# An audio tower on one core: feature-major tensors by batch, folds in place, residual from ScalarE, other buffers at the end

## Chip, cores and metric

The kernel runs on one core of one Trainium2 chip. The metric is device time in microseconds, from the runs of the whole kernel; the profile is that of one further execution. Engines are named as in the profile: PE (TensorE, matmuls), DVE (VectorE), ACT (ScalarE), POOL (GpSimd), SP (SyncE, which here issues DMAs).

## What is computed

64 recordings of 80,000 samples are cut into 157 frames of 512 samples. Each frame is turned by an orthonormal cosine transform (DCT); then come one attention-like layer and one layer of experts, each with a layernorm before it and a residual around it. Cut to what matters:

```python
h = einsum('bfh,kh->bfk', frames, DCT)                   # 64 x 157 x 512
x = layernorm(h)
key, qry = exp(1j*pi*tanh(x @ Wk)), exp(1j*pi*tanh(x @ Wq))   # 4 sets x 8 planes
V = x @ Wv + bv
total = sum over sets: softmax(set_weights)[s] * Re(conj(qry_s) . cumsum_t(key_s * V))
pos   = the same with fixed phases pos * pos_freqs
gate  = sigmoid(x @ Wg + bg)
total = gate * total + (1 - gate) * sigmoid(pos_weight) * pos
h = h + x + (total / norm(t)) @ Wo + bo
y = layernorm(h)
e = argmax_e softmax(mean_t(y) @ rWg + rbg)              # one expert of 16 for a recording
h = h + gate_e * (y @ We[e] + be[e])
```

The cumulative sums are computed as masked products of phases: with 157 positions, scores of 157 x 157 for each recording.

## The kernel before

**Tiles.** The 64 recordings go in 16 groups of 4. A group's 4 x 157 tokens (padded to 160) make five tiles of 128 partitions (NM = 5): four head tiles with the first 128 tokens of one recording each, and one tail tile with the last 32 of all four, of which 29 count (LT). Token-major tiles are 128 x 512; feature-major tensors, which matmuls need as moving or stationary operand, are turned by PE transposes: `transpose_tile` (lines 106 to 111) makes four of them into one PSUM bank and ACT copies the bank into columns of `xT` (L111). Before the change `xT` has 640 columns for each of four feature chunks: 512 of the heads (HEADS) and then 128 of the tails (TAILS).

**Stages of a group g.** `embed` (136 to 165) makes a frame tile into h and x: `fold` (113 to 122) adds and subtracts the mirrored quarters of a frame (`even`, `odd`, then `twice`: L118, L120 and L121 on DVE, L119 on POOL), which halves the DCT's matmuls (L151, L153); `layernorm` (94 to 104) takes the statistics on DVE (L97, L99), the square root on ACT (L101), and then the reciprocal and x on DVE (L103, L104). L157 makes the residual h + x on DVE out of PSUM, and L158 adds the output bias on POOL. `values` (167 to 176) makes V. `phases` (276 to 293) makes keys and queries: 8 matmuls with the weights standing and 512 or 128 columns moving (L284), tanh, sine. `gates` (295 to 312) is the same with 4 x 8 matmuls of 512 or 116 columns (L306) and a sigmoid after each half (L311). `attend` (314 to 369) makes scores (L320, L325), the weighted sums (L345 of 314 columns, L354), the gating (L330, L331), the output product (L131 with `wo`), the residual (L364) and the second layernorm. `turn_x2` (371 to 376) transposes that into `x2T`, of which there is one buffer. `pick` (378 to 445) sums the router's logits over tokens (L388, L396), chooses an expert on DVE, and has POOL gather four weight matrices of 1 MB (L437). `experts` (447 to 484) multiplies (L131, and L465 for the tail tile, four narrow column groups side by side), adds a gathered bias (L453, L473), scales, adds the residual (L476) and writes: L480 for a head tile, 128 rows, and L483 for the tail tile, four DMAs of 29 rows each.

**What sets the order.** Each engine works through its queue in order, and so does SP, which issues all plain DMAs. The engines' order isn't the text's alone: Tile builds it, and moves instructions up where their operands allow it. Buffers come from rings: PSUM has three pairs of banks (`psum`, tag mm) and two single banks (`bank`, tag tr); `frame` has 5 buffers, `even` one, `odd` and `twice` two, `x` three (shared with the outgoing `o`), `we` four, `be` two. A write into a ring's buffer waits for the last reader of what was there. So the frame loads of group g+2 (L81) go out as soon as the folds of group g+1 have read their frames, while PE is in the gates and the attention of group g; `embed(g+1)` is interleaved there with `gates(g)` and `attend(g)`, a tile at a time:

```python
        phases(g)
        next(picks, None)
        if g > 0:
            done(values(g))
        done(picks)
        next(ahead, None)
        for _ in gates(g):
            next(ahead, None)
        attend(g, ahead)
```

The experts of group g-1 follow, then `turn_x2(g)`. At the end (lines 509 to 518) the experts of group 14 begin with the tail tile, then `turn_x2(15)` and `pick(15)` are called between its tiles, and `experts(15)` takes tiles 0 to 3 and then the tail tile.

Of the kernel before, what the change touches and what calls it, by code (L numbers as in the profile page):

```python
# [13 lines left out]
F32 = mybir.dt.float32  # L14
# [7 lines left out]
P = 128  # L22
C = D // P
GB = 4
# [5 lines left out]
HEADS, TAILS = slice(0, GB * P), slice(GB * P, NM * P)  # L30
# [9 lines left out]
def audio_tower(ctx: ExitStack, tc: tile.TileContext, a, out):  # L40
# [16 lines left out]
    small = pool("small", 4)  # L57
# [8 lines left out]
    def psum():  # L66

        return ps_mm.tile([P, 2, 512], F32, tag="mm", name="mm")
# [25 lines left out]
    def layernorm(x, h):  # L94

        st = small.tile([P, 6], F32, tag="st", name="st")
        nc.vector.bn_stats(st, h)  # L97
        mv = small.tile([P, 2], F32, tag="mv", name="mv")
        nc.vector.bn_aggr(mv, st)  # L99
        sd = small.tile([P, 1], F32, tag="sd", name="sd")  # L100
        nc.scalar.activation(sd, mv[:, 1:2], AF.Sqrt, bias=eps)  # L101
        rstd = small.tile([P, 1], F32, tag="rstd", name="rstd")
        nc.vector.reciprocal(rstd, sd)  # L103
        nc.vector.tensor_scalar(x, h, mv[:, 0:1], rstd, ALU.subtract, ALU.mult)  # L104

    def transpose_tile(xT, m, x):

        tr = bank()
        for c in range(C):
            nc.tensor.transpose(tr[:, c * P : (c + 1) * P], x[:, c * P : (c + 1) * P], ident)  # L110
        nc.scalar.copy(xT[:, :, m * P : (m + 1) * P], tr.rearrange("p (c t) -> p c t", c=C))  # L111

    def fold(ft):

        even = p1.tile([P, 2, P], F32, tag="even", name="even")
        odd = p2.tile([P, 2, P], F32, tag="odd", name="odd")
        twice = p2.tile([P, 2, P], F32, tag="twice", name="twice")
        nc.vector.tensor_tensor(even, ft[:, :2, :], ft[:, 2:, :], ALU.add)  # L118
        nc.gpsimd.tensor_tensor(odd, ft[:, :2, :], ft[:, 2:, :], ALU.subtract)  # L119
        nc.vector.tensor_tensor(twice[:, 0, :], even[:, 0, :], even[:, 1, :], ALU.add)  # L120
        nc.vector.tensor_tensor(twice[:, 1, :], even[:, 0, :], even[:, 1, :], ALU.subtract)  # L121
        return twice, odd
# [13 lines left out]
    def embed(g):  # L136


        xT = p1.tile([P, C, NM * P], F32, tag="xT", name="xT", bufs=2)
        res = []  # L140
        pending = None
        S[g] = dict(xT=xT, res=res)
        folded = {0: fold(frames.pop((g, 0)))}
        for m in range(NM):
            h = psum()[:, 0, :]
            twice, odd = folded.pop(m)
            if m + 1 < NM:
                folded[m + 1] = fold(frames.pop((g, m + 1)))
            quarter = h.rearrange("p (r j) -> p r j", r=4)
            for i in range(2):  # L150
                nc.tensor.matmul(quarter[:, 2 * i, :], twice[:, i, :], dct_e[:, i, :], start=True, stop=True)  # L151
            for i in range(2):
                nc.tensor.matmul(quarter[:, 1::2, :], odd[:, i, :], dct_o[:, i, :], start=(i == 0), stop=(i == 1))  # L153
            x = p2.tile([P, D], F32, tag="x", name="x", bufs=3)
            layernorm(x, h)
            r = p1.tile([P, D], F32, tag="res", name="res", bufs=3 * NM)
            nc.vector.tensor_tensor(r, h, x, ALU.add)  # L157
            nc.gpsimd.tensor_tensor(r, r, bo, ALU.add)  # L158
            res.append(r)
            if pending is not None:  # L160
                transpose_tile(xT, *pending)
            pending = (m, x)
            yield
        transpose_tile(xT, *pending)
        yield

    def values(g):

        s = S[g]
        s["v"] = []  # L170
        for m in range(NM):
            ps = by_tokens(psum()[:, 0, :], lambda c: s["xT"][:, c, m * P : (m + 1) * P], wv)
            vt = p1.tile([P, D], F32, tag="v", name="v", bufs=NM)
            nc.vector.tensor_tensor(vt, ps, bv, ALU.add)  # L174
            s["v"].append(vt)
            yield


    first = embed(0)
# [65 lines left out]
    kf = const.tile([P, NM * P], F32, name="kf", tag="kf")  # L245
    qf = const.tile([P, GB, LP], F32, name="qf", tag="qf")
    nc.gpsimd.memset(kf[2 * F :], 0.0)
    nc.gpsimd.memset(qf[2 * F :], 0.0)
    rows = slice(2 * F, 2 * F + 2 * PLANES)
    for i in range(GB):  # L250
        nc.vector.tensor_copy(kf[rows, i * P : (i + 1) * P], pf[:, :P])
        nc.vector.tensor_copy(kf[rows, GB * P + TL * i : GB * P + TL * (i + 1)], pf[:, P:])
        nc.vector.tensor_scalar(qf[rows, i, :], pf, sigp[: 2 * PLANES], -1.0, ALU.mult, ALU.mult)
# [21 lines left out]

    def phases(g):

        xT = S[g]["xT"]
        u = p1.tile([P, NM * P], F32, tag="tT", name="u")
        ps = psum()  # L280
        for k, cols in enumerate((HEADS, TAILS)):
            n = cols.stop - cols.start
            for c in range(C):
                nc.tensor.matmul(ps[:, k, :n], wkq[:, c, :], xT[:, c, cols], start=(c == 0), stop=(c == C - 1))  # L284
            nc.scalar.activation(u[:, cols], ps[:, k, :n], AF.Tanh, bias=bkq)
        nc.vector.scalar_tensor_tensor(u, u, sgn, u, ALU.mult, ALU.max)
        rows = slice(0, 2 * F)
        nc.scalar.activation(kf[rows], u[rows], AF.Sin, bias=off[rows], scale=scl[rows])
        rows = slice(2 * F, P)
        for cols, t, at in ((HEADS, P, slice(0, P)), (TAILS, TL, slice(P, LP))):  # L290
            ub = u[rows, cols].rearrange("p (b t) -> p b t", t=t)
            nc.scalar.activation(qf[: 2 * F, :, at], ub, AF.Sin, bias=off[rows], scale=scl[rows])
        nc.vector.tensor_scalar(qf[: 2 * F], qf[: 2 * F], wvec, None, ALU.mult)

    def gates(g):

        s = S[g]
        xT = s["xT"]
        s["gT"] = gT = p1.tile([P, C, GB, LP], F32, tag="gT", name="gT")
        for o in range(C):  # L300
            ps = psum()
            for k in range(2):
                for c in range(C):
                    moving = xT[:, c, HEADS] if k == 0 else by_tail(xT[:, c, TAILS])
                    n = GB * P if k == 0 else GB * LT
                    nc.tensor.matmul(  # L306
                        ps[:, k, :n], wg[:, c, o * P : (o + 1) * P], moving, start=(c == 0), stop=(c == C - 1)
                    )
                t, at = (P, slice(0, P)) if k == 0 else (LT, slice(P, L))
                pb = ps[:, k, :n].rearrange("p (b t) -> p b t", t=t)  # L310
                nc.scalar.activation(gT[:, o, :, at], pb, AF.Sigmoid, bias=bg[:, o : o + 1])  # L311
            yield

    def attend(g, between):
# [5 lines left out]
        nc.tensor.matmul(ps[:, :P], kf[:, TAILS], qf[:, :, P:], start=True, stop=True)  # L320
        nc.vector.tensor_tensor(tails[:, :, 0, :], by_tail(ps[:, :P]), mask_t, ALU.mult)

        def scores(i):
            ps = bank()
            nc.tensor.matmul(ps[:, :L], kf[:, i * P : (i + 1) * P], qf[:, i, :L], start=True, stop=True)  # L325
            nc.vector.tensor_tensor(att[i % 2][:, 0, :], ps[:, :L], mask, ALU.mult)  # L326
# [41 lines left out]
        for k in ("xT", "v", "gT"):  # L368
            del s[k]

    def turn_x2(g):

        s = S[g]
        s["x2T"] = xT = p1.tile([P, C, NM * P], F32, tag="x2T", name="x2T")
        for m in range(NM):
            transpose_tile(xT, m, s["x2"][m])

    def pick(g):
# [5 lines left out]
        for part, n, first in ((ps[:, :P], P, 0), (ps[:, P:L], LT, GB * P)):  # L384
            for c in range(C):
                for b in range(GB):
                    at = first + b * (P if first == 0 else TL)
                    nc.tensor.matmul(  # L388
                        part[TL * b : TL * (b + 1)],
                        rwg[:, c, :],  # L390
                        xT[:, c, at : at + n],
                        start=(c == 0),
                        stop=(c == C - 1),
                    )
# [52 lines left out]
    def experts(g, order):  # L447
# [3 lines left out]
        for m in order:  # L451
# [8 lines left out]
            if m < GB:  # L460
                by_tokens(ps, lambda c: xT[:, c, m * P : (m + 1) * P], ws[m])
            else:
                for c in range(C):
                    for i in range(GB):
                        nc.tensor.matmul(  # L465
                            ps[TL * i : TL * (i + 1), :],
                            xT[:, c, GB * P + TL * i : GB * P + TL * (i + 1)],
# [11 lines left out]
            if m < GB:  # L479
                nc.sync.dma_start(out=out[GB * g + m, :P, :], in_=o)  # L480
            else:
                for i in range(GB):
                    nc.sync.dma_start(out=out[GB * g + i, P:, :], in_=o[TL * i : TL * i + LT, :])  # L483
# [5 lines left out]
    for g in range(NG):  # L489
# [4 lines left out]
        phases(g)  # L494
        next(picks, None)
# [22 lines left out]
    done(experts(NG - 1, range(NM)))  # L518
# [92 lines left out]
```

## Time and profile before

| | us |
|---|---|
| median of 3 runs | 1660.39 (1660.22 to 1661.74) |
| the profiled execution, device time | 1660.9 |
| its span, first to last instruction | 1659.1 |
| PE busy | 1592.7 |
| DVE busy | 937.4 |
| ACT busy | 545.1, of which table loads at L101 119.3 and at L311 98.8 |
| POOL busy | 326.6 |
| a middle group (638.20 to 738.73) | 100.53 |
| in it, DCT of the next group, gates and attention (738.73 to 779.40) | 40.67, PE busy 38.98 |

The profile gives for each group of instructions the line, the engine, output and inputs by name, the shape, the count, the busy time, the mean of one, and the idle time before it with what ended it. Ends of matmuls are modelled, so the spacing of their starts says more than their busy time. `mm<-wv,xT` reads: tile mm written from wv and xT. A wait is written as who waited, for whom: total us, times, longest. The timeline gives start, length, engine, line, count; SPq and POOLq are the queues that only issue. In the table by windows the columns are the length, then the busy time and the count of PE, weight loads, DVE, ACT and POOL, the granted PE clock, the busy share of the 16 DMA engines, and GB/s.

### The profile page before, as it was taken

To read this page: it belongs to the slowest core of one execution; us is meant where nothing else is said; L and a number is where in the kernel's file an instruction comes from. 1 tells how busy PE (TensorE), PEld (TensorE's weight loads), DVE (VectorE), ACT (ScalarE), POOL (GpSimd) and SP (SyncE) were. 2 spreads that over 40 slices of the span, in tenths; PEclk is the share of its full clock that TensorE was granted. 3 is DMA by queue.
4 is the path that set the end of the run, shared out by engine and by line. 5 is a ranking of instruction groups with operands and counts; after the bars stand their busy time and mean duration, and the time that the engine had idled before them with its cause. 6 is when DMAs were issued, how large, how long until landed. Compare 5 with 4: busy or idle time off the path is not lost. (4 is left out here: it accounts for less than half of the span.)

```text
span 1659.1 us, 18042 instructions
## 1 busy us (share of the span) xinstructions
PE 1592.7 (96%) x6724; PEld 875.5 (53%) x6724; DVE 937.4 (56%) x2162; ACT 545.1 (33%) x769; POOL 326.6 (20%) x377
## 2 busy tenths in 40 slices
PE   7999999999999999999999999999999999999984
PEld 4555556464554645556454554645546455564531
DVE  6556647466463755747466474755637556464452
ACT  3634143251522515134250432515224251342110
POOL 3203112031120403103031120312104031030102
PEclk9999999999999999999999999999999999999997
DMA  5104113141211413013141121413114130121314
GB/s 188 32 1 146 31 56 110 51 146 45 104 48 51 146 48 136 25 45 140 51 146 36 64 97 51 146 45 116 36 51 146 49 136 18 36 112 51 114 50 164
DMA packets 41206, 135.40 MB, mean 82 GB/s; under 512 B 6224, under 2 KB 6624, under 8 KB 32544
## 3 DMA queue, kind: packets, MB, share of 16 engines
q0 software_dynamic: 15616, 88.09, 15.3%
q1 hardware_dynamic: 25504, 46.17, 8.2%
q8 instruction: 53, 0.87, 0.2%
q14 instruction: 33, 0.27, 0.0%
HBM read 113.67 MB, written 20.58 MB: 81 GB/s over the span
## 5 line engine op out<-in xcount | busy, mean ns | idle before, releaser
L306 PE MATMUL mm<-xT,wg 128*128 128x512 f32 (+1 forms) x1024 | 299.9, 438 | 10.0 <-DVE res L157 9.1
L131 PE MATMUL mm<-wv,xT 128*128 128x512 f32 x640 | 283.9, 598 | 3.6 <-ACT xT L111 3.6
L131 PE MATMUL mm<-we,x2T 128*128 128x512 f32 x512 | 225.2, 598 | 10.9 <-DMA we<-in_we,rows 10.9
L131 PE MATMUL mm<-wo,tT 128*128 128x512 f32 x512 | 222.3, 592 | 0.0
L306 PEld LDWEIGHTS mm<-xT,wg 128*128 128x128 f32 x1024 | 156.3, 192 | 114.0 <-issue 92.2
L131 PEld LDWEIGHTS mm<-wv,xT 128*128 128x128 f32 x640 | 119.4, 191 | 142.5 <-issue 137.2
L101 ACT ACT_TABLE_LOAD x93 | 119.3, 1283 | 215.7 <-DVE mv L99 213.5
L131 PEld LDWEIGHTS mm<-we,x2T 128*128 128x128 f32 x512 | 98.2, 192 | 134.3 <-issue 116.3
L119 POOL TENSOR_TENSOR odd<-frame 128x256 f32<-128x256 f32 x80 | 61.3, 767 | 501.2 <-issue 491.9
L131 PEld LDWEIGHTS mm<-wo,tT 128*128 128x128 f32 x512 | 97.3, 190 | 117.2 <-issue 111.0
L453 POOL DMA_INDIRECT be<-in_be,expi x80 | 76.4, 955 | 412.8 <-DVE o L476 404.8
L174 DVE TENSOR_TENSOR v<-mm,bv 128x512 f32<-128x512 f32 x80 | 55.4, 692 | 174.9 <-PE mm L131 174.9
L345 PE MATMUL mm<-att,v 128*128 128x314 f32 x512 | 149.1, 434 | 2.3
L111 ACT COPY x2T<-tr 128x512 f32<-128x512 f32 x80 | 43.7, 588 | 260.0 <-PE tr L110 243.5
L158 POOL TENSOR_TENSOR res<-res,bo 128x512 f32<-128x512 f32 x80 | 101.5, 1278 | 137.1 <-DVE res L157 121.6
L473 DVE TENSOR_TENSOR be<-mm,be 128x512 f32<-128x512 f32 x80 | 55.3, 692 | 126.2 <-PE mm L131 75.4
L101 ACT ACTIVATE sd<-mv,eps 128x1 f32<-128x1 f32 x160 | 47.2, 295 | 207.5 <-DVE mv L99 205.5
L345 PEld LDWEIGHTS mm<-att,v 128*128 128x128 f32 x512 | 92.5, 190 | 39.5 <-DVE att L326 5.7
L110 PE MATMUL tr<-ident,x 128*128 128x128 f32 x640 | 93.4, 277 | 16.4 <-DVE x L104 15.5
L110 PEld LDWEIGHTS tr<-ident,x 128*128 128x128 f32 x640 | 73.8, 141 | 59.1 <-DVE x L104 24.2
L311 ACT ACT_TABLE_LOAD x77 | 98.8, 1283 | 1.3
L476 DVE SCALAR_TENSOR_TENSOR o<-be,gate,res 128x512 f32<-128x512 f32 x80 | 92.9, 1162 | 4.8 <-DMA out<-o 2.0
(105 smaller groups left out, 1793.8 us busy)
## 6 DMA issues: line engine op xcount, KB each, us to landing
frame<-in_frames SPq DMA_DIRECT2D x80, 256.0 KB
out<-o SPq DMA_DIRECT2D x64, 256.0 KB
out<-o SPq DMA_DIRECT2D x64, 58.0 KB
be<-in_be,expi POOLq DMA_INDIRECT x80, 4.1
wv<-in_wv SPq DMA_DIRECT2D x1, 1024.0 KB
wg<-in_wg SPq DMA_DIRECT2D x1, 1024.0 KB
wo<-in_wo SPq DMA_DIRECT2D x1, 1024.0 KB
we<-in_we,rows POOLq DMA_INDIRECT x64, 8.7
```

The costliest lines, as they stand in the source:

```text
L101: nc.scalar.activation(sd, mv[:, 1:2], AF.Sqrt, bias=eps)
L110: nc.tensor.transpose(tr[:, c * P : (c + 1) * P], x[:, c * P : (c + 1) * P], ident)
L119: nc.gpsimd.tensor_tensor(odd, ft[:, :2, :], ft[:, 2:, :], ALU.subtract)
L131: nc.tensor.matmul(ps, lhs(c), w[:, c, :], start=(c == 0), stop=(c == C - 1))
L158: nc.gpsimd.tensor_tensor(r, r, bo, ALU.add)
L174: nc.vector.tensor_tensor(vt, ps, bv, ALU.add)
L306: nc.tensor.matmul(ps[:, k, :n], wg[:, c, o * P : (o + 1) * P], moving, start=(c == 0), stop=(c == C - 1))
L311: nc.scalar.activation(gT[:, o, :, at], pb, AF.Sigmoid, bias=bg[:, o : o + 1])
L345: nc.tensor.matmul(ps[:, c, : 2 * L], v[i][:, cols], att[i % 2], start=True, stop=True)
L453: nc.gpsimd.indirect_dma_start(out=be, out_offset=None, in_=a["be"], in_offset=bass.IndirectOffsetOnAxis(ap=expi[:, m : m + 1], axis=0),)
L473: nc.vector.tensor_tensor(be, ps, be, ALU.add)
L476: nc.vector.scalar_tensor_tensor(o.rearrange("p (j r) -> p r j", r=4), by_r(be), gate[:, m : m + 1], by_r(h), ALU.mult, ALU.add)
```

## The change

- `xT` and `x2T` become [chunk, recording, 160]: a recording's head and tail columns lie together. `transpose_tile` writes the tail tile's columns to four places. For `values`, which needs the 128 tail tokens side by side as a stationary operand, a second copy of them is made (`xT_t`); `kf` gets a tail copy (`kf_t`) too. `xT` and `x2T` share one ring of three buffers.
- `phases`, `gates` and `pick` move two recordings at a time, 2 x 157 = 314 columns (157 for one recording in `pick`), with one activation for both halves.
- `fold` writes its results over the frame instead of into `odd` and `twice`, and is called for all five tiles of the next group right after `phases(g)` (for group 0 at the start); `even` has two buffers.
- The residual h + x is made on ACT from x as mean + x * (sd + 1); POOL makes sd + 1. `small` has six buffers.
- The tail tile's rows are written in two DMAs for each recording, 16 and 13 rows. The last group's tiles go in the order 0, 1, tail, 2, 3.

```diff
-    def transpose_tile(xT, m, x):
+    def transpose_tile(xT, m, x, apart=None):
         tr = bank()
         ...
-        nc.scalar.copy(xT[:, :, m * P : (m + 1) * P], tr.rearrange("p (c t) -> p c t", c=C))
+        if m < GB:
+            nc.scalar.copy(xT[:, :, m, :P], tr.rearrange("p (c t) -> p c t", c=C))
+            return
+        nc.scalar.copy(xT[:, :, :, P:], tr.rearrange("p (c b t) -> p c b t", c=C, b=GB))
+        if apart is not None:
+            nc.scalar.copy(apart, tr.rearrange("p (c t) -> p c t", c=C))

     def fold(ft):
-        even = p1.tile([P, 2, P], F32, tag="even", name="even")
-        odd = p2.tile([P, 2, P], F32, tag="odd", name="odd")
-        twice = p2.tile([P, 2, P], F32, tag="twice", name="twice")
+        even = p2.tile([P, 2, P], F32, tag="even", name="even")
         nc.vector.tensor_tensor(even, ft[:, :2, :], ft[:, 2:, :], ALU.add)
-        nc.gpsimd.tensor_tensor(odd, ft[:, :2, :], ft[:, 2:, :], ALU.subtract)
-        nc.vector.tensor_tensor(twice[:, 0, :], even[:, 0, :], even[:, 1, :], ALU.add)
-        nc.vector.tensor_tensor(twice[:, 1, :], even[:, 0, :], even[:, 1, :], ALU.subtract)
-        return twice, odd
+        nc.gpsimd.tensor_tensor(ft[:, :2, :], ft[:, :2, :], ft[:, 2:, :], ALU.subtract)
+        nc.vector.tensor_tensor(ft[:, 2, :], even[:, 0, :], even[:, 1, :], ALU.add)
+        nc.vector.tensor_tensor(ft[:, 3, :], even[:, 0, :], even[:, 1, :], ALU.subtract)
     ...
     def embed(g):
-        xT = p1.tile([P, C, NM * P], F32, tag="xT", name="xT", bufs=2)
+        xT = p1.tile([P, C, GB, LP], F32, tag="xT", name="xT", bufs=3)
+        tails = p1.tile([P, C, P], F32, tag="xT_t", name="xT_t")
         ...
-            layernorm(x, h)
+            mean, sd = layernorm(x, h)
+            sd1 = small.tile([P, 1], F32, tag="sd1", name="sd1")
+            nc.gpsimd.tensor_scalar(sd1, sd, 1.0, None, ALU.add)
             r = p1.tile([P, D], F32, tag="res", name="res", bufs=3 * NM)
-            nc.vector.tensor_tensor(r, h, x, ALU.add)
+            nc.scalar.activation(r, x, AF.Identity, bias=mean, scale=sd1)
             nc.gpsimd.tensor_tensor(r, r, bo, ALU.add)
     ...
     def gates(g):
             for k in range(2):
                 for c in range(C):
-                    moving = xT[:, c, HEADS] if k == 0 else by_tail(xT[:, c, TAILS])
-                    n = GB * P if k == 0 else GB * LT
                     nc.tensor.matmul(
-                        ps[:, k, :n], wg[:, c, o * P : (o + 1) * P], moving, start=(c == 0), stop=(c == C - 1)
+                        ps[:, k, : 2 * L],
+                        wg[:, c, o * P : (o + 1) * P],
+                        xT[:, c, 2 * k : 2 * k + 2, :L],
+                        start=(c == 0),
+                        stop=(c == C - 1),
                     )
     ...
     def turn_x2(g):
-        s["x2T"] = xT = p1.tile([P, C, NM * P], F32, tag="x2T", name="x2T")
+        s["x2T"] = xT = p1.tile([P, C, GB, LP], F32, tag="xT", name="x2T", bufs=3)
     ...
             else:
                 for i in range(GB):
-                    nc.sync.dma_start(out=out[GB * g + i, P:, :], in_=o[TL * i : TL * i + LT, :])
+                    for lo, hi in ((0, TL // 2), (TL // 2, LT)):
+                        nc.sync.dma_start(
+                            out=out[GB * g + i, P + lo : P + hi, :], in_=o[TL * i + lo : TL * i + hi, :]
+                        )
     ...
         phases(g)
+        for m in range(NM):
+            if g + 1 < NG:
+                fold(frames[g + 1, m])
     ...
-    done(experts(NG - 1, range(NM)))
+    done(experts(NG - 1, [0, 1, GB, 2, 3]))
```

In the instruction order that is built from the changed text, the folds of group g+2 stand among the DCTs of group g+1 (in the stage of `gates(g)`), on DVE each `even` ahead of the reciprocal and x of the tile whose DCT freed the frame's buffer; each frame load waits for that DCT on PE. At the end the transposes of group 15 stand between the matmuls of tile 0 of group 14, and its router ahead of tile 1.

## The prediction

> **What bounds the kernel now.** I read the busy shares first, then who TensorE (PE) waits for, then PE's timeline over one middle group, then the end.
>
> ```profile
> PE 1592.7 (96%) x6724; PEld 875.5 (53%) x6724; DVE 937.4 (56%) x2162; ACT 545.1 (33%) x769; POOL 326.6 (20%) x377
> ```
>
> ```profile
> PE tr L110 <- DVE x L104: 15.5, 16, 1.9
> PE mm L131 <- DMA we<-in_we,rows: 10.9, 1, 10.9
> PE mm L306 <- DVE res L157: 9.1, 15, 0.6
> PE mm L151 <- DVE twice L120: 6.4, 1, 6.4
> ```
>
> PE is the bound. It waits for about 50 us in all, partly in a pattern that returns in each group of 100.5 us (0.64 + 0.90 + 0.15 us), partly once, at the start and at the end. Timeline of PE in one group:
>
> ```profile
> 746.25 4.56 PE L306 MATMUL mm<-xT,wg 128*128 128x512 f32 x16 [0.64 <-DVE res L157]
> ...
> 753.46 3.60 PE L306 MATMUL mm<-xT,wg 128*128 128x512 f32 x8
> 756.89 0.61 PE L151 MATMUL mm<-dct_e,twice 128*128 128x128 f32 x4
> ...
> 765.42 0.66 PE L110 MATMUL tr<-ident,x 128*128 128x128 f32 x4 [0.90 <-DVE x L104]
> ...
> 766.13 1.05 PE L306 MATMUL mm<-xT,wg 128*128 128x116 f32 x8
> 767.02 0.71 PE L325 MATMUL tr<-qf,kf 128*128 128x157 f32 x4
> ...
> 774.12 5.45 PE L345 MATMUL mm<-att,v 128*128 128x314 f32 x20
> 779.40 13.90 PE L131 MATMUL mm<-wo,tT 128*128 128x512 f32 x32
> ```
>
> Starts divided by counts give the true spacing: (756.89-753.46)/8 = 0.429 us for 512 columns, (767.02-766.13)/8 = 0.111 for 116, (779.40-774.12)/20 = 0.264 for 314. (Each fp32 matmul of the code is two such instructions.) The end, on PE, DVE and SP, and DMA share over 1648 to 1657:
>
> ```profile
> 1608.31 1.15 PE L110 MATMUL tr<-ident,x 128*128 128x128 f32 x8 [0.68 <-ACT x2T L111]
> ...
> 1623.48 16.80 PE L131 MATMUL mm<-we,x2T 128*128 128x512 f32 x32 [10.95 <-DMA we<-in_we,rows]
> 1640.21 3.64 PE L465 MATMUL mm<-we,x2T 128*32 128x512 f32 x32
> ```
>
> ```profile
> 1645.12 1.12 DVE L476 SCALAR_TENSOR_TENSOR o<-be,gate,res 128x512 f32<-128x512 f32 x1
> ```
>
> ```profile
> 1646.27 1.41 SPq L483 DMA_DIRECT2D out<-o  x4
> ```
>
> ```profile
> 1648.00:1657.00 9.00, 0.00 (x0) 0.00 (x0) 0.00 (x0) 0.00 (x0) 0.00 (x0) 0.50 0.07 23
> ```
>
> The last arithmetic ends at 1646.24, the span at 1659.1: 12.9 us in which 7% of the DMA engines work.
>
> [...] 0.07 is about 1/16, and the packet records show 4 x 29 packets of 2 KB in series, 0.08 us each (9.3 us). [...] the frame load issued at 741.36 lands its packets at 742.58 to 743.69; one issued at 753.82, with four expert gathers under way, at 757.26 to 759.90, when the gathers end (759.82). [...] an L120 that takes 0.28 us alone took 1.91 beside two L158 of POOL:
>
> ```profile
> 751.30 1.91 DVE L120 TENSOR_TENSOR twice<-even 128x128 f32<-128x128 f32 x1 [1.69 <-PE mm L151]
> ```
>
> ```profile
> 750.50 2.49 POOL L158 TENSOR_TENSOR res<-res,bo 128x512 f32<-128x512 f32 x2
> ```
>
> [...] the new residual needs no ACT_TABLE_LOAD (1283 ns); the built order has none, as L111's copy has none now.
>
> **The change part by part**, against the profiled execution: 1660.9 us, of which the span is 1659.1 (the median of the runs is 1660.4).
>
> Equal streams. Gates: 512 pairs of 0.429+0.111 become 2 x 0.264: 13 ns x 512 = -6.7. Phases: 128 pairs, -1.7. Router (L388): the 64 instructions of a group take 1.30 us (719.24 to 720.54); 157 columns in eight rounds at about 0.133 (L325's spacing) give 1.07: -3.7 in 16 groups. All on PE: **-12.1**. Scores of the tails (116 for 128 columns): nothing. The merged activations save ScalarE 4 x 0.27 us a group; it is a third busy, nothing.
>
> Residual. DVE loses 80 x 684 ns (L157), which also ended the 0.64 us wait, since h is now free after x. ScalarE gains one operation (0.6 to 0.7 us, as L311 or L111) that waits for x, POOL one of 128x1 (0.1 to 0.2). Queued behind it on ScalarE are the next square root and a copy of xT.
>
> Folds. They write into the frame, so a frame's buffer is free only after PE's DCT of it, not after the fold. The built order moves the folds of group g+2 into the same stage: even(m) of the new frame stands on DVE ahead of the reciprocal and x(m) that PE's transposes need. Frame loads are thus on the path. Walked in the old clock from 738.73, with DCT 1.31, transposes 0.44, gates 16 x 0.264 = 4.22: without waits DCT 1 and 2 end at 745.8 and 751.8, and transposes 1, 2, 3 are due at 751.8, 757.7, 763.7. Gathers are issued from 745.0. Load 1, issued 745.95, lands at 750.4 (behind one gather) to 753 (behind two); then even 0.42, reciprocal 0.16, x 0.81 and hand-overs, 1.65 in all: 752 to 754.7, a wait of 0.3 to 2.9. Load 2, issued 751.95, lands at 754.7 free, at 758.6 if it shares, at 759.8 if it ends with the gathers as the one of 753.82 did: x(2) at 756.4, 760.25 or 761.45 for a due time of 757.7: total delay 0, 2.5 or 3.7. The fold's adds then meet two L158-like adds on POOL (2.5 us), which puts x(3) at 766.8 to 767.4, just at its delayed due time. Load 4 (free: 2.33 us to the last packet as at 741.36, 2.75 with the hand-overs) plus 2.15 (the 1.65 and a gate product) makes 4.9 after the last DCT; PE's next use of that PSUM buffer is 3.9 later: another 1.0. With the walk's end at 8.6 us after that, the stage of 40.67 us becomes 38.5, 41.0 or 42.0. Measured against its matmul time (38.98-0.42), waits W are 0, 2.4 or 3.4 where there were 1.69. I take 2.4 (sharing): 13 groups x 0.71 = **+9.2**. Group 14 has no frames to load: -1.7; group 0 no gathers: about **-1**.
>
> Head. All five folds (each even 0.43, POOL 0.77, two adds 0.28, in part serial) stand before the first statistics on DVE: 13.5 for 10.9 us. The extra ScalarE steps add about 0.3 a tile: **+3.5** (1 to 5).
>
> End. x2T no longer waits for the last reader (the wait at 1608.31), so transposes and router lie among the tiles of group 14. From the end of the tail tile (1592.8): the router's sum at 10.4 us, choices on DVE, mixed with three output steps and a wait for tile 2, at 18.7, gathers issued at 19.2 and landed 5.7 later (1617.77 to 1623.44) at 24.9 for 30.7 now. The tiles then end at 43.8 for 51.05; the last one is a 128-row tile: DVE 1.95, issue and flight about 2.4, closing 1.3: 49.4 for 66.3. **-17** (12 to 20). Splitting 29 rows as 16+13 adds 64 issues on SP, 0.35 us each; behind them on SP are only the next frame loads, due 25 us later.
>
> Sum: -12.1+9.2-1.7-1+3.5-17 = -19: 1641 beside the median.
>
> **Rivals.** Late: load 2 always ends with the gathers (W 3.4): 13 x 1.71 = +22, in all -6, 1655. For it: the load of 753.82. Against: load 2 comes 1.9 us earlier. Prompt: loads slip in between gathers and W is 0: -22, in all -50, 1611. [...] against: the same packets. Slower than before: the frame load is held past the bias gathers too (their packets end at 765.0), DVE's queue stands still until 763.3, W about 8, 13 x 6.3 = +82, in all 1715. It decides from W = 1.69 + 28.3/13 = 3.9. For it: one in-order queue serves fold, norm and PSUM release; against: the load of 762.88 had its last packet 2.8 us later beside those gathers (765.66). That the streams aren't shorter can't be: their spacing is measured.
>
> **Numbers.** Forecast 0.5 (own range 1632 to 1650), late 0.2, prompt 0.2, slower 0.1. 0.2% (3.3 us) is about what a measurement can tell from no change. The likely case is faster, late nearly always; prompt too: faster 0.8, same 0.08, slower 0.12. 1612 to 1660 leaves out the slower case and part of the prompt one.
>
> **What would show it.** Spacing 0.264 in gates and phases; no PE wait for L157; PE waits at the transposes released by x, DVE's even waiting for frame loads in groups 1 to 13 and not in 14; the gather wait near 1623 down to 8 us or less; the last DMA landing within 4 us of the last DVE step. No waits at even, or waits over 3.9 us a group, would make the forecast wrong.

## The result, and the profile after

The changed kernel takes 1670.72 us (median of 4 runs, 1668.95 to 1677.66), the kernel before 1660.31 beside it: ratio 1.0069, 95% interval 1.004 to 1.0098. The change makes it slower by 0.7%, where 1641 was forecast. The profiled execution took 1668.95, its span 1667.2 us. On the page PE is less busy than before and DVE too:

```profile
PE 1583.6 (95%) x6212; PEld 919.6 (55%) x6212; DVE 866.6 (52%) x2082; ACT 550.1 (33%) x753; POOL 345.3 (21%) x458
```

So work went away, and waiting came. The waits view (who waited for what: us in total, times, longest):

```profile
DVE even L123 <- DMA frame<-in_frames: 149.5, 32, 7.1
...
PE tr L111 <- DVE x L103: 47.1, 31, 3.1
...
PE mm L135 <- DMA we<-in_we,rows: 8.4, 1, 8.4
...
PE tr L346 <- DVE att L347: 5.8, 14, 0.4
PE tr L346 <- DVE att_t L340: 5.6, 15, 0.4
```

The wait for the residual is gone. The transposes wait 47.1 us for x (15.5 before), and DVE, which makes x, stands 149.5 us for frames. In the kernel before it stood once, for the first frame:

```profile
DVE even L118 <- DMA frame<-in_frames: 4.3, 1, 4.3
```

Two small waits at the scores (L346) are new. PE's timeline of one group:

```profile
759.78 1.03 PE L155 MATMUL mm<-dct_o,frame 128*128 128x256 f32 x4
762.91 1.02 PE L111 MATMUL tr<-ident,x 128*128 128x128 f32 x4 [2.10 <-DVE x L103]
763.73 5.75 PE L322 MATMUL mm<-xT,wg 128*128 128x314 f32 x16
...
771.06 4.39 PE L322 MATMUL mm<-xT,wg 128*128 128x314 f32 x16
...
778.22 0.54 PE L346 MATMUL tr<-qf,kf 128*128 128x157 f32 x2 [0.37 <-DVE att_t L340]
779.17 0.54 PE L346 MATMUL tr<-qf,kf 128*128 128x157 f32 x2 [0.41 <-DVE att L347]
...
790.78 13.90 PE L135 MATMUL mm<-wo,tT 128*128 128x512 f32 x32
```

The same 16 gate products take 4.39 us, and 5.75 just after the wait of 2.10. The table of stretches (the last three numbers are the granted clock, the DMA share and GB/s) shows that PE's clock is halved there (0.50); the DMA engines are full in the same stretch (1.01). Three of the groups 1 to 13 have such a stretch, and this is one of them.

```profile
762.50:764.00 1.50, 1.08 (x5) 1.09 (x6) 1.15 (x3) 0.03 (x1) 0.00 (x0) 0.69 1.01 426
764.00:766.00 2.00, 2.00 (x5) 1.25 (x5) 0.00 (x0) 1.97 (x3) 0.00 (x0) 0.50 1.01 420
```

DVE in the same group: after the statistics it stands for the fold's first add, and reciprocal and x come right behind it: x begins at 762.05, 6.27 us after the statistics' end (755.78).

```profile
755.60 0.18 DVE L98 BATCH_NORM_AGGREGATE mv<-st 128x2 f32<-128x6 f32 x1
761.51 0.42 DVE L123 TENSOR_TENSOR even<-frame 128x256 f32<-128x256 f32 x1 [5.74 <-DMA frame<-in_frames]
761.86 0.16 DVE L102 RECIPROCAL rstd<-sd 128x1 f32<-128x1 f32 x1
762.05 0.81 DVE L103 TENSOR_SCALAR x<-mm,mv,rstd 128x512 f32<-128x512 f32 x1
```

That frame load was issued at 754.89 and had its packets at 757.6 to 761.0, among those of the expert gathers; a load with nothing beside it, issued at 749.36, had them at 750.3 to 751.8. In the kernel before, a first add came 23 to 95 us after the issue of its load (from the third group's frames on), so that even a slow load had landed; in the changed kernel it comes 2.6 to 9.1 us after.

The end, on PE, DVE and SP, and the stretch after DVE's last step (1664.15 to 1667.2; its DMA share 0.23 for 0.07): the gather wait is 8.41 us, and the span ends 3.0 us after DVE.

```profile
1641.59 9.84 PE L135 MATMUL mm<-we,x2T 128*128 128x512 f32 x16 [8.41 <-DMA we<-in_we,rows]
```

```profile
1663.02 1.13 DVE L491 SCALAR_TENSOR_TENSOR o<-be,gate,res 128x512 f32<-128x512 f32 x1
```

```profile
1661.45 3.07 SPq L495 DMA_DIRECT2D out<-o  x2
```

```profile
1664.10:1667.20 3.10, 0.00 (x0) 0.00 (x0) 0.05 (x1) 0.00 (x0) 0.00 (x0) 0.51 0.23 85
```

Where the 8.1 us between the two spans came from, by PE's first output projection of each group:

| stretch | before | changed | difference |
|---|---|---|---|
| start to group 0's output projection | 93.35 | 89.12 | -4.2 |
| from there to group 14's | 1389.2 | 1416.9 | +27.7 |
| group 15 | 89.4 | 88.5 | -0.9 |
| last output projection to the end | 87.1 | 72.6 | -14.5 |

In a group, the time from the output projection to the router's total goes from 59.83 to 59.61. The rest, from that total to the next output projection, is called the stage below: 40.7 us before, of which PE waits 1.69; 43.14 in the changed kernel (mean of groups 1 to 13), of which it waits 4.22.

### The profile page after: what moved, and what is told of

The parts are those of the page before. It is cut to its first block, busy times and chain, and to the rows that moved or that the text cites. A ratio compares the mean times of both kernels' runs of the same rounds, so it can differ in the third digit from the quotient of the medians.

```text
span 1667.2 us, 17202 instructions
## 1 busy us (share of the span) xinstructions
PE 1583.6 (95%) x6212; PEld 919.6 (55%) x6212; DVE 866.6 (52%) x2082; ACT 550.1 (33%) x753; POOL 345.3 (21%) x458
## 4 chain that ended last, share of the span: by engine, by line
PE 83%; DMA 6%; DVE 6%; issue 3%; POOL 1%; ACT 1%; SPq 0%; POOLq 0%; DVEq 0%; ACTq 0%
PE mm L135 45%; PE mm L322 10%; PE mm L366 8%; DMA frame<-in_frames 6%; PE mm L297 4%; PE tr L111 4%; PE mm L480 3%; PE mm L155 2%; PE mm L375 2%; DVE x L103 2%; PE tr L346 2%; DVE frame L125 1%; PE mm L153 1%; PE tr L407 1%; POOL frame L124 1%
## 5 line engine op out<-in xcount | busy, mean ns | idle before, releaser
L322 PE MATMUL mm<-xT,wg 128*128 128x314 f32 x1024 | 283.6, 430 | 0.0
L322 PEld LDWEIGHTS mm<-xT,wg 128*128 128x128 f32 x1024 | 191.0, 190 | 70.7 <-issue 2.1
L135 PE MATMUL mm<-wv,xT 128*128 128x512 f32 x512 | 225.8, 598 | 2.0 <-ACT xT L113 2.0
L100 ACT ACTIVATE sd<-mv,eps 128x1 f32<-128x1 f32 x160 | 47.1, 295 | 389.5 <-DVE mv L98 388.1
L135 PEld LDWEIGHTS mm<-wv,xT 128*128 128x128 f32 x512 | 96.1, 191 | 120.7 <-issue 117.6
L366 PE MATMUL mm<-att,v 128*128 128x314 f32 x512 | 144.5, 430 | 0.0
L111 PE MATMUL tr<-ident,x 128*128 128x128 f32 x640 | 94.9, 279 | 47.7 <-DVE x L103 47.1
L160 POOL TENSOR_SCALAR sd<-sd 128x1 f32<-128x1 f32 x80 | 18.4, 230 | 566.8 <-ACT sd L100 532.0
L123 DVE TENSOR_TENSOR even<-frame 128x256 f32<-128x256 f32 x80 | 36.7, 460 | 149.6 <-DMA frame<-in_frames 149.5
L113 ACT COPY x2T<-tr 128x512 f32<-128x512 f32 x64 | 34.4, 589 | 231.4 <-PE tr L111 231.4
L385 DVE TENSOR_TENSOR res<-mm,res 128x512 f32<-128x512 f32 x80 | 55.3, 691 | 80.8 <-PE mm L135 80.8
```

The source lines that it names most:

```text
L135: nc.tensor.matmul(ps, lhs(c), w[:, c, :], start=(c == 0), stop=(c == C - 1))
L322: nc.tensor.matmul(ps[:, k, : 2 * L], wg[:, c, o * P : (o + 1) * P], xT[:, c, 2 * k : 2 * k + 2, :L], start=(c == 0), stop=(c == C - 1),)
L366: nc.tensor.matmul(ps[:, c, : 2 * L], v[i][:, cols], att[i % 2], start=True, stop=True)
L385: nc.vector.tensor_tensor(res[m], ps, res[m], ALU.add)
```

## The experiments

The theory: the fold in place makes each frame load start only after PE's DCT of the tile before it in that buffer. The load lands late, the fold's first add stands for it on DVE, and x, behind it in the same queue, comes late to PE. Rival explanations: A, the residual on ScalarE delays what is queued behind it; B, the fold's own steps; C, the new streams; D, late landing in itself.

| kernel | median us | to before (95%) | stage, mean of groups 1 to 13 | waits in it |
|---|---|---|---|---|
| before | 1660.3 to 1661.0 | 1 | 40.7 | 1.69 |
| changed | 1670.72 | 1.0069 (1.004 to 1.0098) | 43.14 | 4.22 |
| e1: 7 frame buffers | 1672.01 | 1.0067 (1.0053 to 1.0081) | 43.08 | 4.08 |
| e2: folds apart | 1611.65 | 0.9704 (0.9691 to 0.9718) | 38.73 | 0.79 |
| e3: before + folds alone | 1727.66 | 1.0395 (1.0381 to 1.0409) | 45.98 | 4.90 |
| e4: no expert gathers from group 8 | 1655.5 (one run) | - | below | below |
| e5: frames held longer | 1613.78 | 0.9718 (0.9705 to 0.9732) | 38.74 | 0.79 |
| e6: before + end alone | 1648.4 | 0.9925 (0.9911 to 0.9939) | 40.87 | 1.69 |
| e7: before + residual alone | 1643.23 | 0.9895 (0.988 to 0.9911) | 39.65 | 1.32 |
| e8: before + streams alone | 1638.85 | 0.9867 (0.9852 to 0.9882) | 39.52 | 1.53 |
| e9: changed, residual on DVE | 1709.82 | 1.0302 (1.0287 to 1.0318) | 45.95 | 5.01 |
| e10: e2 once more | 1610.19 (one run) | - | 38.73 | 0.79 |
| e11: e2, scores early | 1601.92 | 0.9645 (0.9632 to 0.9658) | 38.05 | 0.50 |
| e12: before + row split alone | 1656.6 | 0.9973 (0.9964 to 0.9983) | 40.87 | 1.69 |

(For e6 to e12, but e9, the stage is that of a middle group; it hardly varies.)

**e1, more frame buffers.**

```
-            ft = p1.tile([P, C, P], F32, tag="frame", name="frame", bufs=NM)
+            ft = p1.tile([P, C, P], F32, tag="frame", name="frame", bufs=NM + 2)
```

> Changed kernel with 7 frame buffers in place of 5, nothing else; the built order of PE and ScalarE is the same, on DVE and POOL only a few steps at the start move. Theory (a frame buffer comes free only after PE's DCT, so frame loads start late, land behind the expert gathers, and hold DVE, which keeps x from PE): loads now start two tiles earlier, DVE no longer waits for frames, the waits at the transposes of x (3.3 us a group in 13 groups) and the slow-clock stretches (1.5 us each, three of them) go, the two score waits (0.37 + 0.41 us) stay: 1671 - 43 - 4 = 1624, range 1617 to 1634. Rival A (the residual on ScalarE delays the square root and the copies): 1665 to 1672. Rival B (the fold's own steps on DVE and POOL, [...] sit ahead of the norm): order unchanged, so 1662 to 1672.

A miss: nothing changed. The waits view shows nearly the same line:

```profile
DVE even L123 <- DMA frame<-in_frames: 149.1, 33, 6.7
```

The few steps that move at the start, which I had noted and passed over, are the reason. Two more loads and two more folds go out there, and from then on the folds run two frames further ahead: each first add again belongs to the load just issued (issued at 658.28, add at 664.55 after 5.40 us of waiting). A deeper ring didn't take the newest load off DVE's queue: an add still comes 2.6 to 9.2 us after its load's issue. So this run doesn't speak against the theory, nor for it; another way was needed (e5).

**e2, folds apart** (the old fold, called in embed one tile ahead; all else as changed).

```
...
-        nc.gpsimd.tensor_tensor(ft[:, :2, :], ft[:, :2, :], ft[:, 2:, :], ALU.subtract)
-        nc.vector.tensor_tensor(ft[:, 2, :], even[:, 0, :], even[:, 1, :], ALU.add)
...
+        nc.gpsimd.tensor_tensor(odd, ft[:, :2, :], ft[:, 2:, :], ALU.subtract)
+        nc.vector.tensor_tensor(twice[:, 0, :], even[:, 0, :], even[:, 1, :], ALU.add)
...
-            ft = frames.pop((g, m))
+            twice, odd = folded.pop(m)
+            if m + 1 < NM:
+                folded[m + 1] = fold(frames.pop((g, m + 1)))
...
-        for m in range(NM):
-            if g + 1 < NG:
-                fold(frames[g + 1, m])
```

> Changed kernel with the folds of before (into buffers of their own, inside the embedding, one tile ahead); streams, residual, x2T buffer, row copies and last order as changed. Theory: frames are freed by the fold, loads go early, 3.3 us a group and the slow-clock stretches go; up to 0.9 us a group may come back at the transpose of x (as before): 1671 - 47 + 0 to 12 = 1624 to 1636, best 1628. Rival A (residual on ScalarE): 1663 to 1672, since that is untouched. Rival C (new streams make the loss, for instance by the copy of the tail tokens): 1660 to 1672.

1611.65, better than the range: the 0.9 us wait didn't come back. What is left in the stage are the two score waits.

```profile
PE 1570.0 (98%) x6212; PEld 920.6 (57%) x6212; DVE 861.9 (54%) x2082; ACT 545.6 (34%) x753; POOL 343.9 (21%) x458
```

```profile
PE tr L349 <- DVE att_t L343: 5.9, 15, 0.7
PE tr L349 <- DVE att L350: 5.8, 14, 0.4
DVE even L124 <- DMA frame<-in_frames: 4.2, 1, 4.2
```

The folds as changed thus cost 1670.7 - 1611.7 = 59 us; 13 x (43.14 - 38.73) = 57 of it lie in the stages. A and C are out as the cause: both are untouched here. The change to the folds has two sides, writing in place and being called ahead, and no run takes one without the other.

**e3, folds alone** (the other corner: before, with the new fold and its calls as in the change, nothing else).

```
-            twice, odd = folded.pop(m)
-            if m + 1 < NM:
-                folded[m + 1] = fold(frames.pop((g, m + 1)))
+            ft = frames.pop((g, m))
...
         phases(g)
+        for m in range(NM):
+            if g + 1 < NG:
+                fold(frames[g + 1, m])
```

> Kernel before with the folds in place and moved, and nothing else. Theory: waits of 4 us a group or more in groups 1 to 13 in place of 1.69, DVE having the residual adds besides: 13 x 2.5 to 3.5 more, some 4 us less in group 0, some slow-clock stretches: 1660 + 30 = 1690, range 1680 to 1705. Rivals A and C: the folds are innocent, 1655 to 1663.

1727.66, 67 us more than before and above the range. The sign is right, the size was too small: besides waits of 4.90 us, halved clock falls into each of groups 1 to 13.

**e4, no expert gathers from group 8 on**; later groups use group 7's weights, so part of the computation is left out.

```
+        if g >= 8:
+            s.update(ws=S["ws"], gate=gate, expi=expi)
+            yield
+            return
         ws = []
```

> Changed kernel that leaves out the gathers of expert weights from group 8 on and uses group 7's weights there (the other gathers, of biases, stay). Theory: frame loads are late because they share the DMA engines with the gathers: stages from score to scores in which no gathers go out become 42.7 - 3.3 = 39.4 us, earlier stages stay at 42.7. If only the late start of the loads mattered, and not what they meet, the stages would stay above 41.5. Rivals A and B: 42.7 everywhere.

Half a miss. The five stages without gathers (groups 9 to 13) all have waits of 2.5 to 3.0 us for 4.2, but four of them, with halved clock, still take 42.2 to 42.7; the last, without it, takes 40.67, above the 39.4 of the theory. PE and ScalarE in one of them:

```profile
1069.39 0.66 PE L111 MATMUL tr<-ident,x 128*128 128x128 f32 x4 [0.76 <-DVE x L103]
...
1084.74 0.89 PE L346 MATMUL tr<-qf,kf 128*128 128x157 f32 x2 [1.62 <-ACT xT L113]
1085.42 3.63 PE L366 MATMUL mm<-att,v 128*128 128x314 f32 x8
```

```profile
1069.43 0.81 ACT L162 ACTIVATE res<-x,mv,sd 128x512 f32<-128x512 f32 x1 [4.12 <-DVE x L103]
1070.26 1.28 ACT L330 ACT_TABLE_LOAD   x1
1071.56 0.79 ACT L330 ACTIVATE gT<-mm,bg 128x628 f32<-128x628 f32 x1
```

Without the gathers a load's add still comes 4.2 us after its issue (1062.72, add at 1066.91), and two bias gathers go at the same time; DVE stands 3.31 us, but x is only 0.76 late. Yet ScalarE, where the new residual waits for x ahead of the sigmoid of the gates and the next square root, stays behind to the end of the stage, and PE pays 1.62 at a copy of xT; the eight products after it take 3.63 us for 2.28, at halved clock. So gathers make the loads later, the theory's 3.3 at the transposes shrinks as it should, but late x has a second way to PE: rival A is right that far, as an amplifier of a late x.

**e5, frames held longer.** The decisive one: loads go out later than in the changed kernel, not earlier, and the folds are still in place.

```
-            ft = frames.pop((g, m))
+            ft = frames[g, m]
...
         attend(g, ahead)
+        if g + 1 < NG:
+            tick = small.tile([P, NM], F32, tag="tick", name="tick")
+            for m in range(NM):
+                nc.gpsimd.tensor_tensor(tick[:, m : m + 1], frames.pop((g + 1, m))[:, 0, :1], S[g]["x2"][0][:, :1], ALU.add)
```

> Changed kernel, folds in place as changed, but five one-column additions on GpSimd read each frame together with the first x2 of the group, so a frame's buffer comes free only after the attention's output projection has begun: loads go out about 25 us later than in the changed kernel, and in the built order the folds then stand on DVE after the stage, no longer ahead of the reciprocals and x. Theory (what costs is DVE standing in order at the fold's first add for a load that has just been issued; the lateness alone costs nothing): no frame wait in the stage, stage 38.7 us for 42.7, no slow-clock stretches: 1671 - 13 x 4 - 4 = 1615, range 1606 to 1625. Rival D (late landing itself is the cost, later loads cost more): 1675 to 1720. Rival A (residual on ScalarE): 1662 to 1672.

1613.78, within 2 us of the folds apart. Loads go out at 768.50 to 770.42, after the stage (output projection at 761.76); PE's waits at the transposes are down to the start of the kernel:

```profile
DVE even L123 <- DMA frame<-in_frames: 16.8, 21, 4.3
...
PE tr L111 <- DVE x L103: 3.9, 2, 2.5
```

Here too an add comes 2.6 to 7.2 us after its load's issue, and DVE stands for some of them, up to 4.3 us. But these adds stand among the steps of the second layernorm, and PE, in the output product and the experts, waits for nothing there. So neither the fold in place (B) nor late landing (D) costs: what costs is where the first add stands on DVE, ahead of the reciprocals and x that PE needs next, with a load issued a moment before.

**e6, e7, e8: the other three parts, each alone on the kernel before.** e6 and e7 take the end's and the residual's lines of the change as they are; e8 takes all of its tensor layouts and streams.

> Kernel before with only the end changed: x2T takes a third buffer of xT's, the 29 rows go as 16 + 13, the last tiles run 0, 1, tail, 2, 3. The prediction's step: -17, so 1644; the changed kernel's trace has 72.6 us from the last output projection to the end for 87.1: -14.5, so 1646.5. If the gain came with the streams or folds instead: above 1655.

> Kernel before with only the residual moved to ScalarE. Theory: the 0.64 us wait of each group goes; the 0.90 us at a transpose of x goes too if x comes 0.68 us earlier on DVE: 1661 - 15 x 0.64 = 1651 to 1661 - 15 x 1.9 = 1633, best 1642. Rival A (the ScalarE step delays square roots and copies): 1661 or more.

> Kernel before with only the new tensors and streams of 314 columns (folds, residual, end as before). The prediction's step: -12.1, so 1649. If the two score waits (0.37 + 0.41 us for 0.15) that the changed kernel has come with the streams, since no gate stream stands between tail scores and scores any more: 1649 + 15 x 0.6 = 1658. Rival C (streams or the copy of the tails make the loss): above 1661.

-12.3, -17.5 and -21.9 us: all three gain, and the sign of the whole is the folds'. With e3's +66.7 they add up to +15.0, and together they give +10.4. That doesn't make the parts independent: e9 shows two differences that nearly cancel. In e6 the last stretch (output projection to end) falls from 87.1 to 73.1 us, but each stage is 0.2 us longer at the same waits; e12 shows why.

e7 comes near its best value, 1642, but not on its ground, so that part is luck: the wait of 0.64 us goes, the 0.90 at the transpose of x stays. The stage is 1.05 us shorter all the same, more than the wait's length, and group 0's output projection comes 4.0 us earlier. e8 is better than both values said: the waits of 0.64 and 0.90 go, and two of 0.46 and 1.07 come at the scores. So waits at the scores do come with the streams.

**e9, the residual back on DVE in the changed kernel.**

```
-            mean, sd = layernorm(x, h)
+            layernorm(x, h)
...
-            nc.scalar.activation(r, x, AF.Identity, bias=mean, scale=sd1)
+            nc.vector.tensor_tensor(r, h, x, ALU.add)
```

> Changed kernel with only the residual back on VectorE (h + x, ahead of the 0.68 us that the next steps wait). Theory: with the folds in place, DVE's queue is what the transposes wait for, so 0.68 us more a tile there makes it worse; from the separate runs (folds alone 1727.7, streams alone -21.9, end alone -12.3) 1693, range 1680 to 1705. Rival A (the ScalarE residual, queued for x ahead of the gates' sigmoid and the square root, is part of the loss): 1660 or less.

1709.82: 39 us more than the changed kernel, and 17 over the sum of the separate runs, above the range. The residual is worth 17.5 us by itself and 39 when DVE's queue is what PE waits for: that is 21.5 more, which the 17 nearly cancel in the sum of the four parts. That ends rival A as a cause: an amplifier of late x, it gains more than it costs.

**e10 and e11, the score waits.** e10 is e2 once more. e11 is e2 with this:

```
-        for _ in gates(g):
-            next(ahead, None)
+        for o, _ in enumerate(gates(g)):
+            next(ahead, None)
+            if o == 2:
+                early(g)
```

The new function early holds the tail scores and scores(0), taken out of attend as they are.

> The version with folds apart once more, beside the next one: 1611, stage 38.73 us with two score waits of 0.37 and 0.41.

> Version with folds apart, and the tail scores and the first scores of each group issued before the last gate block, so that gate products stand between them and the masks on VectorE that free their PSUM banks. If the two waits are only missing cover: 15 x (0.78 + up to 0.2 of refilling) = 12 to 15 less than 1611.6: 1597 to 1600. If they come from VectorE being late whatever the order: 1609 to 1613.

1601.92, the fastest: 9.7 us less than e2 (8.3 less than the one run of e10) for 12 to 15 expected. Both waits go, and one of 0.50 us comes at the tails' products (att_t). The waits were missing cover (other work for PE while DVE makes what it needs next): in the changed kernel no gate product is left between tail scores and scores.

**e12, the row split alone.**

```
-                    nc.sync.dma_start(out=out[GB * g + i, P:, :], in_=o[TL * i : TL * i + LT, :])
+                    for lo, hi in ((0, TL // 2), (TL // 2, LT)):
+                        nc.sync.dma_start(
+                            out=out[GB * g + i, P + lo : P + hi, :], in_=o[TL * i + lo : TL * i + hi, :]
+                        )
```

> Kernel before with only the four copies of 29 rows split into 16 + 13; the last tile stays the tail tile. In the profile of before the four copies are issued in 1.41 us and then take 9.3 us of packets in series on one engine, after which the span ends 1.3 us later. [...] eight issues of 0.38 us (3.0) replace 1.41 and the packets take about 1 us after the last: 1660.4 + 1.6 - 8.5 = 1653.5, range 1651 to 1656. The rest of the end's -12.3 us (e6) then belongs to the x2T buffer and the order. If the split changes no engine count: 1660 to 1664.

1656.6, just above the range. The span ends 5.9 us after DVE's last step for 12.9, -7.0 as worked out (SP issues eight copies in 3.23 us; that the packets of the split rows would overlap was my estimate, and the last section has what came); the 0.2 us a stage of e6 is here too and takes 13 x 0.2 = 2.6 back. The traces show where it comes from. x shares its three buffers with the outgoing o, so before DVE writes an x it waits for the copies out of that buffer. Where these are the tail tile's, once a group in 13 groups, two semaphore instructions stand on DVE between the reciprocal and x for four copies, and four for eight, 0.1 us each. So x begins 0.24 us after the reciprocal for 0.05, h + x behind it ends about 0.2 us later, and the gate products that wait for h + x begin as much later.

```profile
1648.53 3.23 SPq L484 DMA_DIRECT2D out<-o  x8
```

## Why the prediction was wrong

**The step that failed** is the fold's: "I take 2.4 (sharing): 13 groups x 0.71 = +9.2". By the same measure (stage less 38.56 us of matmuls) the waits W are 43.14 - 38.56 = 4.58, and 13 x (4.58 - 1.69) = +37.6: 28 us missed, all of the distance between -19 and +8 and a little more. Its parts:
- 3.4 us at the transposes of x. The mechanism was as told, DVE even standing for loads in groups 1 to 13 and not in 14; and the loads landed within the walk (load 1 by 13.9 us after the stage's start for 11.7 to 14.3, load 2 by 20.8 for 19.9 or 21.1). But of the outcomes written down, all of them estimates of how the load meets the gathers, sharing with 2.4 was preferred to "late" with 3.4, on the ground that load 2 comes 1.9 us earlier. It does, and its add still began only 1.3 us before the last gather had landed (769.63). The further 1.0 us that the walk had for load 4 didn't come: no stage has a wait of PE for that PSUM buffer.
- 0.78 us at the scores. The prediction said of the tail scores "nothing". The count of columns was right; that 116-column gate products had stood between the tail scores (L320) and the scores (L325) before the change, and would not any more, was not asked. e11 shows this part.
- 0.34 us of halved clock (three stretches of 1.4 to 1.5 us in 13 groups). The walk had one clock.

These parts come to 4.5 because two things cancel: a stage without waits at the transposes takes 37.95 us besides its waits, not 38.56, and waits cost about as much beyond their own length (see the last section).

The rival on the slower side had the right place (DVE's in-order queue), but wanted W near 8 through the bias gathers; its own point of decision, 3.9, was passed, but not by way of the bias gathers. The upper end of the range, 1660, came from "late"; with the scores (13 x 0.78) and the clock (13 x 0.34) added, "late" becomes -6 + 10 + 4 = +8, about what was measured.

**Streams, -12.1.** Right in kind: 0.264 us in gates and phases. In a quiet group of the changed kernel gates take 16.92 for 17.54 us, phases 4.33 for 4.45, the router 1.20 for 1.30: -0.84 x 16 = -13.4. The router gives -0.10, not -0.23: eight rounds of 157 columns take 0.150 each, not L325's 0.133. Alone the streams give -21.9: transposes (4.83 to 4.44 us a group) and DCT products (4.57 to 4.32) get shorter too, and so does group 0's stage, and the list of waits holds none of this. That it comes from fewer alternations in PE's order and fewer waits was not shown.

**Residual.** Its wait went, as said, with no table load at the new step, which takes 0.81 us for 0.6 to 0.7 said. That nothing else would come of 80 x 684 ns on DVE was too careful: -17.5 alone (e7), 39 in the changed kernel (e9).

**Head +3.5 and group 0 -1.** The phases begin 0.9 us later (45.46 for 44.52); then group 0's stage, with waits of 1.58 for 3.64 us and without the halved clock it had before (16 gate instructions in 6.23 us at 65.04), gives 5 back: -4.2 where +2.5 less the streams was said.

**Group 14, -1.7.** Its stage is 38.73 for 39.95: it had only 1.06 of waits to lose, and keeps the score waits.

**End -17.** -14.5, within 12 to 20. From the tail tile's end (1615.4) gathers are issued at 19.8 (19.2 said), landed at 26.1 (24.9), tiles end at 46.6 (43.8), all at 51.8 (49.4). Of the 2.8 by which the tiles end later than said, 1.2 are the later gathers; behind the wait of 8.41 the clock is halved (9.84 us for 16 products, 7.03 ahead of it), as it was at this place in the kernel before (16.80 for 32). The gather wait is just above the 8 said; the span ends 3.0 us after DVE's last step, within 4. That the 16 + 13 rows cost something in the stages (e12), the prediction had at nothing; in the changed kernel it is seen in one stage only.

What stays open: why the clock is halved after some waits and not others (below), and how much of the folds' cost the place of the calls alone would bring, without writing in place.

## What to carry to other kernels

Before a buffer is reused in place, ask which load that delays, and then which queue its first reader stands in: an add of 0.4 us, waiting for its load ahead of work that PE needed, cost 57 us here in 13 groups. A deeper ring didn't help while the reader moved ahead with it (e1, 1672.01 us); loading later, with the reader out of the way, did (e5, 1613.78). When a stream is merged or moved, look at what had stood between its neighbours: it can be the cover of their waits (e11, 9.7 us). Where copies out of a buffer are split, the next writer of the buffer has more of them to wait for (e12, 0.2 us a stage). A gain that is bound to an engine's queue (the residual) is worth what that queue is worth, 17.5 or 39 us.

## What the hardware showed

- PE's clock was halved (0.50 granted) in stretches of 3.41 us, or several such in a row, on a fixed grid: in the changed kernel they start 191, 28, 185, 71 and 8 times 3.413 us after one another; behind the gather wait of 8.41 us there are three in a row (10.24 us). The three in groups 1 to 13 came after windows of that length in which PE had waited 2.0, 2.1 and 2.5 us in all; in all other windows, from 100 us after the start to 60 us before the end, it had waited 1.9 at most. In e3 the 13 stages with halved clock have it after windows of 1.7 to 2.4, with 1.7 the most elsewhere; in e9 (1.5 to 2.7, and up to 1.8) and e4 (1.4 to 2.9, and up to 1.9) the two overlap. So it is a tendency, and no run tests it alone.
- A wait cost PE more than its length in the profile: a stage of the changed kernel without slow clock has 38.4 us besides its waits with waits at two transposes, 38.6 with three, 37.95 with none: about 0.2 us for each. The profile counts a wait from the modelled end of the matmul ahead of it, so some of this may be its way of counting.
- The packets of the four copies of 29 rows came one after another, most of them 0.08 us apart (before, 116 packets from 1647.01 to 1657.80). With 16 + 13 rows those of one copy came together: the 16 of the first start within 0.32 us (1658.57 to 1658.89 in the changed kernel), the 13 of the second within 0.29 (1658.99 to 1659.28). The span ends 5.9 us after DVE's last step for 12.9 (e12 and before).
- Each pair of copies that DVE had to wait for took it one semaphore instruction, 0.1 us: x began 0.24 us after the reciprocal with eight copies and 0.05 with four (e12 and before).
